# Two edits in a fused graph network: one operation for a complex product, and the sums of h made ahead

## The chip, the cores and the metric

The kernel runs on one core of a Trainium2 chip. The metric is the device time of one execution in microseconds. A core has five engines with instruction queues of their own: TensorE (matmuls; its weight loads are listed apart), VectorE, ScalarE, GpSimd and SyncE, which issues most of the DMA. They are tied together by semaphores. In the profile they are PE, PEld, DVE, ACT, POOL and SP.

## The reference

x has 128 graphs of 128 nodes with 256 channels; everything is float32. Two layers follow each other, and each adds its result to x. Before each, h is the layer norm of x with negative values set to zero.

Layer 0 (the part that the change touches), for each graph:

```python
h1     = relu(bn1(conv1(h)))                   # 1 tap
x_conv = relu(bn2(conv2(h1)) + h)              # 17 taps, 256 -> 256 channels
A      = exp(-dist(h @ w_se.T + b_se)) * mask
x_nmp  = A @ relu(h @ w_msg.T + b_msg)
gi     = concat(x_conv, x_nmp) @ w_ih.T + b_ih
gh     = h @ w_hh.T + b_hh
r, z   = sigmoid(gi_r + gh_r), sigmoid(gi_z + gh_z)
n      = tanh(gi_n + r * gh_n)
x      = x + (1 - z) * n + z * h
```

Layer 1 is a graph convolution over five fixed groups of the first 25 nodes, with 512 hidden channels, twice per group, summed with softmax weights.

## The kernel before, in words

The 128 graphs are worked on in 32 groups q of four. The 17-tap convolution is done by a Fourier transform over pieces of the node axis: F = 48 values a piece, NB = 4 pieces a graph, so that 32 graphs make 128 pieces, one batch. There are four batches of eight groups each.

The work is cut into stages, written as generators.

- **tap_weights** (once) turns the 17 taps of conv2 into 48 matrices of 256x256, by a matmul with the constant `tap` (made on the host in `_fourier`, lines 86 to 89), and stores them in memory as `wfd`. For a frequency f from 1 to 23, slice f and slice 24 + f are the two stored parts of its complex weight.
- **stage_a(q)** normalizes, transposes, makes h (`hTa`, stored in memory as `hTd`), applies conv1 and takes the forward transform into `X`: for each f a real and an imaginary part, X[:, k, 2f] and X[:, k, 2f + 1].
- **stage_b(bat)** multiplies in the frequency domain, for f from 0 to 23 (lines 506 to 530). Frequencies 1 to 23 need a complex product. It is done with three real ones: Xr·Vr and Xi·Vi into the two halves of the PSUM tile `pa`, and (Xr + Xi)·(Vr + Vi) into `pb`. The two sums are made on GpSimd (`add`, lines 494 and 495). ScalarE copies `pa` to SBUF (`pac`, line 519), and three VectorE operations give the real part, Xr·Vr - Xi·Vi, and the imaginary part (lines 523 to 525). `y` goes to memory (`yd`). There are 92 such products.
- **stage_n(q)** loads h of a group, computes the affinity and `x_nmp` (`neighbours`). For the first eight groups this was done ahead, in `early(q)`, beside stage_b(0); for these stage_n only loads the result.
- **stage_c(q)** makes the inverse transform (line 673) and `xc` (lines 676 to 679), and then the gates. The gates' matrix products use a fast scheme with seven products for eight blocks, whose operands are sums of quarter blocks. `sums` (lines 546 to 554) makes four such operands with four VectorE subtractions of 128x256: `th` from h, `tm` from x_nmp, `tc` from xc. They are used from line 730 on. At its end GpSimd combines z, n and h (lines 791 to 796).
- **prepare(blk)** and **block(blk)** are layer 1, for blocks of 16 graphs.

**Order.** Instructions are written out by `Order.run`: it takes steps from lanes of generators, by the lanes' weights and by due times that each step yields. The order of each engine's queue is fixed by it, and an engine runs its queue strictly in order. stage_b(0) runs beside `early` and the folding of the gate weights on GpSimd (`fold_gates`). After that one lane holds stage_n and stage_c of all groups, two at a time; beside it run stage_a and stage_b of the next batches, and when these are through, layer 1.

**Where `th` is made.** Line 759, in stage_c(q) behind the second product with `whn`: if stage_n(q + 1) has ended by then, which sets IN[q + 1], the sums of h for group q + 1 are made there. Otherwise line 665 makes them at the head of stage_c(q + 1), ahead of the operations for `xc`.

**Buffers.** `ptmp` is a ring of five PSUM banks, which `pa`, `pb`, the products of the neighbours (`pse`, `pm`, four `pd`, `px`), the transforms (`ph`, `pc`, `pf`, `pi`, `po`) and layer 1 share, in the order in which they are written out. `pgat` is a ring of three banks for the gates. `hT` has two buffers, `th` one.

Of the kernel before, what the change touches and what calls it, by code (L numbers as in the profile page):

```python
# [9 lines left out]
FP = mybir.dt.float32  # L10
AF = mybir.ActivationFunctionType
ALU = mybir.AluOpType
# [3 lines left out]
B, N, D = 128, 128, 256  # L16
# [3 lines left out]
P = 128  # L20
# [9 lines left out]
NF = F // 2 - 1  # L30
# [29 lines left out]
def _fourier():  # L60

    fwd = np.zeros((P, F, NB))
    inv = np.zeros((P, OB * NB // 2))
    tap = np.zeros((TAPS, F))
    i, t = np.arange(OB), np.arange(TAPS)  # L70
    for b in range(NB):
        for u in range(F):
            n = OB * b + u - PAD
            if 0 <= n < N:
                fwd[n, 0, b], fwd[n, 1, b] = 1, (-1) ** u
                for f in range(1, NF + 1):
                    th = 2 * np.pi * ((f * u) % F) / F
                    fwd[n, 2 * f, b], fwd[n, 2 * f + 1, b] = np.cos(th), -np.sin(th)
    for b in range(NB // 2):
        s = slice(b * OB, (b + 1) * OB)  # L80
        inv[b * F, s], inv[b * F + 1, s] = 1 / F, (-1.0) ** i / F
        for f in range(1, NF + 1):
            th = 2 * np.pi * ((f * i) % F) / F
            inv[b * F + 2 * f, s] = 2 / F * np.cos(th)
            inv[b * F + 2 * f + 1, s] = -2 / F * np.sin(th)
    tap[:, 0], tap[:, NF + 1] = 1, (-1.0) ** t
    for f in range(1, NF + 1):
        th = 2 * np.pi * ((f * t) % F) / F
        tap[:, f], tap[:, NF + 1 + f] = np.cos(th), np.sin(th)
    tap4 = np.zeros((P, 64))  # L90
    for r in range(4):
        tap4[32 * r:32 * r + TAPS, :F] = tap
    return fwd.reshape(P, F * NB), inv, tap4
# [114 lines left out]
def kernel(ctx: ExitStack, tc: tile.TileContext, x, adj, consts, vecs, w_se, conv1_w,  # L208
                    conv2_w, w_msg, b_msg, w_ih, w_hh, W1, W2, b2, fusion_w, out):
    nc = tc.nc  # L210
# [27 lines left out]
    def v(name, i=None):  # L238
        a, b = VAT[name]
        return vec[:, a:b] if i is None else vec[:, a + i:a + i + 1]  # L240
# [109 lines left out]
    xf = lab.enter_context(tc.tile_pool(name="xf", bufs=1, side="right"))  # L350
    LATE = {}
    X = xf.tile([P, 2, F, P], FP, name="X")
# [121 lines left out]
    def stage_b(bat):  # L474
        while not all(q in A_DONE for q in range(bat * BQ, (bat + 1) * BQ)):
            yield 0.0, 0.5
        while "xf" not in LATE:
            yield 0.0, 0.5
        if bat == 0:
            yield 0.0, 12.0  # L480
        WF, xf = {}, LATE["xf"]

        def load_w(f):
            w = WF[f] = xf.tile([P, 2, 3, D], FP, tag="wf", name=f"wf{bat}_{f}")
            for k in range(2):
                nc.sync.dma_start(out=w[:, k, :2], in_=wfd[f::NF + 1, k * P:(k + 1) * P]
                                  .rearrange("s p o -> p s o"))

        XS = {}

        def add(f):

            XS[f] = xf.tile([P, 2, P], FP, tag="xs", name=f"xs{bat}_{f}", bufs=2)
            nc.gpsimd.tensor_tensor(XS[f], X[:, :, 2 * f], X[:, :, 2 * f + 1], ALU.add)  # L494
            nc.gpsimd.tensor_tensor(WF[f][:, :, 2], WF[f][:, :, 0], WF[f][:, :, 1], ALU.add)  # L495

        def product(ps, xk, f, s):

            for k in range(2):
                nc.tensor.matmul(ps, xk(k), WF[f][:, k, s], start=(k == 0), stop=(k == 1))  # L500

        for f in range(2):
            load_w(f)
        yield 0.0, 4.0
        late = None
        for f in range(NF + 1):
            if f + 2 <= NF:
                load_w(f + 2)
            if f < NF:
                add(f + 1)  # L510
            y = xf.tile([P, 2, D], FP, tag="y", name=f"y{bat}_{f}")
            pa = ptmp.tile([P, 2, D], FP, tag="tmp", name=f"pa{bat}_{f}")
            for s in range(2):
                product(pa[:, s], lambda k: X[:, k, 2 * f + s], f, s)
            if f == 0:
                nc.vector.tensor_copy(y, pa)
            else:
                pac = xf.tile([P, 2, D], FP, tag="pac", name=f"pac{bat}_{f}", bufs=2)
                nc.scalar.activation(pac, pa, AF.Copy)  # L519
                pb = ptmp.tile([P, D], FP, tag="tmp", name=f"pb{bat}_{f}")  # L520
                xs = XS.pop(f)
                product(pb, lambda k: xs[:, k], f, 2)
                nc.vector.tensor_sub(y[:, 0], pac[:, 0], pac[:, 1])  # L523
                nc.vector.tensor_add(pac[:, 0], pac[:, 0], pac[:, 1])
                nc.vector.tensor_sub(y[:, 1], pb, pac[:, 0])  # L525
            WF.pop(f)
            if late is not None:
                nc.gpsimd.dma_start(out=yd[bat][:, 2 * f - 2:2 * f], in_=late)
            late = y
            yield 1.7 if f == 0 else 2.6, 1.0  # L530
        nc.gpsimd.dma_start(out=yd[bat][:, F - 2:F], in_=late)
        B_DONE.add(bat)


    IN, IN2, X1, N_DONE = {}, {}, {}, set()

    def load_n(q):
        hT = LATE["io"].tile([P, 2, 512], FP, tag="hT", name=f"hT{q}")
        nc.sync.dma_start(out=hT, in_=hTd[q])
        ad = LATE["io"].tile([P, GB, N], FP, tag="adj", name=f"adj{q}")  # L540
        nc.sync.dma_start(out=ad, in_=adj[q * GB:(q + 1) * GB].rearrange("b n m -> n b m"))
        return hT, ad

    TH = {}

    def sums(name, q, x):


        t = LATE["fr"].tile([P, 4, D], FP, tag=name, name=f"{name}{q}")
        nc.vector.tensor_sub(t[:, 0], x[:, 0, D:], x[:, 0, :D])  # L550
        nc.vector.tensor_sub(t[:, 1], x[:, 1, D:], t[:, 0])  # L551
        nc.vector.tensor_sub(t[:, 2], x[:, 1, D:], x[:, 0, D:])
        nc.vector.tensor_sub(t[:, 3], t[:, 1], x[:, 1, :D])
        return t
# [81 lines left out]
    def stage_n(q):  # L636
        if q < BQ:
            hT = LATE["io"].tile([P, 2, 512], FP, tag="hT", name=f"hT{q}")
            nc.sync.dma_start(out=hT, in_=hTd[q])
            xm = LATE["fr"].tile([P, 2, 512], FP, tag="xnmp", name=f"xms{q}", bufs=2)  # L640
            nc.sync.dma_start(out=xm, in_=xmd[q])
            yield 0.0, 4.0
        else:
            while q not in A_DONE:
                yield 0.0, 1.0
            hT, ad = load_n(q)
            yield 0.0, 4.0
            xm = LATE["fr"].tile([P, 2, 512], FP, tag="xnmp", name=f"xnmp{q}", bufs=2)
            yield from neighbours(q, hT, ad, xm)
        IN[q] = hT, xm  # L650

    def stage_c(q):
        while not (q - 1 in G_DONE and q in IN):
            yield 0.0, 0.5
        hT, xm = IN.pop(q)
# [8 lines left out]

        th = TH.pop(q) if q in TH else sums("th", q, hT)
        xc = fr.tile([P, 2, 512], FP, tag="xc", name=f"xc{q}")
        for h in range(2):
            yt = IN2.pop((q, h))
            s = slice(h * D, (h + 1) * D)
# [19 lines left out]
        def part(ps, w, i, xs, first, last):  # L689


            n = [(m, o) for m in range(w.shape[3] // P) for o in xs]
            for j, (m, (k, x, t)) in enumerate(n):
                nc.tensor.matmul(ps[:, m], w[:, i, k, m * P:(m + 1) * P], factor(i, x, t),  # L694
                                 start=first and j == 0, stop=last and j == len(n) - 1)

        def product(w, i, xs):
            ps = bank(w, i)
            part(ps, w, i, xs, True, True)
            return ps  # L700

        def bank(w, i):
            return pgat.tile([P, w.shape[3] // P, D], FP, tag="gat", name=f"p{w.shape[3]}{q}_{i}")
# [48 lines left out]
        for dc in range(2):  # L752
            pg = pgat.tile([P, 512], FP, tag="gat", name=f"pg{q}_{dc}")
            for k in range(2):
                nc.tensor.matmul(pg, whn[:, k, dc * P:(dc + 1) * P], hT[:, k],  # L755
                                 start=(k == 0), stop=(k == 1))
            nc.vector.scalar_tensor_tensor(r[:, dc], pg, v("b_hh", 4 + dc), r[:, dc],
                                           op0=ALU.add, op1=ALU.mult)
            if dc and q + 1 in IN:
                TH[q + 1] = sums("th", q + 1, IN[q + 1][0])  # L760
            yield 1.75, 0.0

        xs = [(1, xm, tm), (0, xc, tcs)]
# [308 lines left out]
    beside = Lane([tap_weights(), fold_embedding()] + [early(q) for q in range(BQ)])  # L1072
    order.run(begin, beside, until=begin)
    order.run(Lane([stage_b(0)]), beside, Lane([fold_gates()]))
    first, second = [], [setup_1()]
    for bat in range(1, NBAT):
        first += [stage_a(q) for q in range(bat * BQ, (bat + 1) * BQ)] + [stage_b(bat)]
# [47 lines left out]
```

## Time and profile before

| | |
|---|---|
| median of 3 runs | 2251.74 us (2242.12 to 2255.31) |
| span of the profiled run | 2239.3 us, mean granted TensorE clock 0.979 |
| TensorE matmul busy | 2151.1 us |
| TensorE weight loads busy | 1759.6 us |
| VectorE busy | 1332.5 us |
| ScalarE busy | 717.7 us |
| GpSimd busy | 809.7 us |
| matmuls of pa and pb (line 500) | 185.7 + 96.2 us |
| line 519 (ScalarE copy of pa) | 54.7 us |
| lines 523, 524, 525 (VectorE) | 55.3 + 75.6 + 39.1 us |
| lines 550 to 553 for th (VectorE) | 23.9 + 35.6 + 38.9 + 39.0 us |

A group of the profile is read like this: line, engine, operation, output<-inputs by the program's names, shapes and number; then busy time in us and the mean of one in ns; then the idle time of the engine just before these instructions, with what ended most of it. A line of the waits names the waiting instruction, what it waited for, the total in us, the number of waits and the longest. A line of the timeline has the start and the length in us and, in brackets, the idle time before it and its releaser. Every float32 matmul of the program stands in the trace as two records: `pa` has 768 records for 96 tiles of four matmuls.

stage_b(0) runs from about 152 to 277 us, the other three passes of stage_b between 450 and 1355 us; layer 1 begins at about 1390 us.

### The profile page before, as it was taken

The numbers are of one execution on the slowest core, as the hardware profiler recorded it, in microseconds if no ns is written. First come the engines' busy times: TensorE is split into PE (matmuls) and PEld (weight loads), VectorE is DVE, ScalarE is ACT, GpSimd is POOL, SyncE is SP. The second block draws the span as 40 slices with busy tenths as digits, with TensorE's granted clock in tenths as the row PEclk, the third lists the DMA queues.
The fourth block names the chain that finished last, engine by engine and source line by source line (L and its number), as shares of the span: only waits on it lengthen the run. The fifth ranks groups of instructions, "written<-read, shape, count | busy, mean of one in ns | idle before, by whom it ended". The sixth has DMA issues, their size and how long they took to land.

```text
span 2239.3 us, 31926 instructions
## 1 busy us (share of the span) xinstructions
PE 2151.1 (96%) x11820; PEld 1759.6 (79%) x11820; DVE 1332.5 (60%) x2843; ACT 717.7 (32%) x1455; POOL 809.7 (36%) x978
## 2 busy tenths in 40 slices
PE   6998999999999999999999998999999999999997
PEld 3577778888888888888888887787877878878775
DVE  4666755666556676666666665565555565655442
ACT  2431223322234332333332332333233333333232
POOL 2325504365533245542225553423323323222320
PEclk9998999999999999999999999999999999999999
DMA  9886633454533344432325444322222222221221
GB/s 187 240 273 201 199 102 104 146 174 145 161 99 98 92 151 146 140 119 80 100 63 173 137 134 135 77 76 76 76 57 86 67 57 79 80 74 37 74 77 48
DMA packets 193982, 259.72 MB, mean 116 GB/s; under 512 B 21981, under 2 KB 157154, under 8 KB 192290
## 3 DMA queue, kind: packets, MB, share of 16 engines
q1 hardware_dynamic: 165682, 175.89, 27.6%
q0 software_dynamic: 27312, 81.03, 11.7%
q8 instruction: 94, 1.54, 0.3%
q10 hardware_dynamic: 832, 0.75, 0.2%
q14 instruction: 62, 0.51, 0.1%
HBM read 178.44 MB, written 79.17 MB: 115 GB/s over the span
## 4 chain that ended last, share of the span: by engine, by line
PE 81%; DVE 8%; DMA 4%; issue 3%; POOL 2%; ACT 2%; SPq 0%; DVEq 0%; POOLq 0%; ACTq 0%
PE p L694 31%; PE pa L500 6%; PE pg L755 5%; PE ph L996 4%; PE pc L396 4%; PE pz L1005 4%; PE pm L591 4%; PE pi L673 4%; PE pf L409 3%; PE pb L500 3%; PE px L616 2%; PE pg L1038 1%; PE py L979 1%; PE ph L383 1%; PE po L807 1%
## 5 line engine op out<-in xcount | busy, mean ns | idle before, releaser
L500 PE MATMUL pa<-wf,X 128*128 128x256 f32 x768 | 185.7, 385 | 4.6 <-DVE y L525 4.6
L791 POOL TENSOR_TENSOR d<-hT,r 128x512 f32<-128x512 f32 x64 | 86.4, 1350 | 242.1 <-ACT r L788 209.4
L278 POOL TENSOR_TENSOR rs<-rs,cst 128x4 f32<-128x4 f32 x40 | 41.2, 1031 | 361.1 <-DVE rs L277 346.4
L500 PEld LDWEIGHTS pa<-wf,X 128*128 128x128 f32 x768 | 146.9, 193 | 29.4 <-DVE y L525 6.3
L694 PE MATMUL p<-tc,wrz 128*128 128x256 f32 x512 | 153.0, 380 | 4.3 <-DVE tc L551 4.3
L694 PE MATMUL p<-tm,wrz 128*128 128x256 f32 x512 | 152.4, 379 | 1.6 <-DVE tm L551 1.6
L694 PE MATMUL p<-th,wrz 128*128 128x256 f32 x512 | 153.7, 382 | 0.0
L396 PE MATMUL pc<-c1w,hTa 128*128 128x256 f32 x512 | 126.8, 392 | 7.9 <-ACT hTa L385 7.9
L495 POOL TENSOR_TENSOR wf<-wf 128x512 f32<-128x512 f32 x92 | 124.6, 1354 | 13.1 <-DMA wf<-wfd 13.0
L494 POOL TENSOR_TENSOR xs<-X 128x256 f32<-128x256 f32 x92 | 69.5, 755 | 162.5 <-PE pb L500 159.1
L673 PEld LDWEIGHTS pi<-cst,yt 96*128 96x128 f32 x1024 | 123.2, 196 | 4.7 <-issue 3.1
L396 PEld LDWEIGHTS pc<-c1w,hTa 128*128 128x128 f32 x512 | 97.8, 195 | 36.8 <-ACT hTa L385 16.0
L673 PE MATMUL pi<-cst,yt 96*128 96x64 f32 x1024 | 121.8, 278 | 2.9 <-DMA yt<-yd 2.9
L755 PE MATMUL pg<-hT,whn 128*128 128x512 f32 x256 | 122.6, 605 | 0.0
L694 PE MATMUL p<-hT,wrz 128*128 128x256 f32 x384 | 121.7, 400 | 0.0
L591 PE MATMUL pm<-wmsg,hT 128*128 128x256 f32 x512 | 121.7, 382 | 0.0
L519 ACT ACTIVATE pac<-pa 128x512 f32<-128x512 f32 x92 | 54.7, 595 | 198.5 <-PE pa L500 194.9
L996 PE MATMUL ph<-yz,w 128*128 128x96 f32 (+3 forms) x640 | 114.4, 335 | 3.4 <-DVE yz L981 2.8
L523 DVE TENSOR_TENSOR y<-pac 128x256 f32<-128x256 f32 x92 | 55.3, 602 | 104.7 <-ACT pac L519 102.2
L591 PEld LDWEIGHTS pm<-wmsg,hT 128*128 128x128 f32 x512 | 96.7, 191 | 24.0 <-issue 10.8
L694 PEld LDWEIGHTS p<-tc,wrz 128*128 128x128 f32 x512 | 96.7, 190 | 20.0 <-DVE tc L551 7.1
L707 ACT ACTIVATE r<-r,brz 128x256 f32<-128x256 f32 x128 | 58.1, 500 | 168.0 <-DVE r L735 155.4
(205 smaller groups left out, 4864.4 us busy)
## 6 DMA issues: line engine op xcount, KB each, us to landing
wf<-wfd SPq DMA_DIRECT2D x192, 256.0 KB, 3.2
yd<-y POOLq DMA_DIRECT2D x96, 256.0 KB, 2.6
yt<-yd SPq DMA_DIRECT2D x64, 384.0 KB, 3.8
hT<-hTd SPq DMA_DIRECT2D x40, 512.0 KB, 6.0
w<-in_W SPq DMA_DIRECT2D x40, 512.0 KB, 3.8
xa<-in_x SPq DMA_DIRECT2D x128, 128.0 KB, 4.3
hTd<-hTa POOLq DMA_DIRECT2D x32, 512.0 KB, 4.6
xt<-in_x SPq DMA_DIRECT2D x128, 128.0 KB, 3.2
```

The source lines that it names most:

```text
L396: nc.tensor.matmul(pc[:, i], hT[:, k, (2 * h + i) * N:(2 * h + i + 1) * N], c1w[:, k], start=(k == 0), stop=(k == 1))
L409: nc.tensor.matmul(pf[:, i, :F * NB], h1[:, 2 * h + i, k * P:(k + 1) * P], fwd, start=True, stop=True)
L494: nc.gpsimd.tensor_tensor(XS[f], X[:, :, 2 * f], X[:, :, 2 * f + 1], ALU.add)
L495: nc.gpsimd.tensor_tensor(WF[f][:, :, 2], WF[f][:, :, 0], WF[f][:, :, 1], ALU.add)
L500: nc.tensor.matmul(ps, xk(k), WF[f][:, k, s], start=(k == 0), stop=(k == 1))
L591: nc.tensor.matmul(pm[:, i], hT[:, k, j * N:(j + 1) * N], wmsg[:, k], start=(k == 0), stop=(k == 1))
L673: nc.tensor.matmul(pc[:, co, a * 64:(a + 1) * 64], yt[:, a, co * P:(co + 1) * P], inv[:HB], start=True, stop=True)
L694: nc.tensor.matmul(ps[:, m], w[:, i, k, m * P:(m + 1) * P], factor(i, x, t), start=first and j == 0, stop=last and j == len(n) - 1)
L755: nc.tensor.matmul(pg, whn[:, k, dc * P:(dc + 1) * P], hT[:, k], start=(k == 0), stop=(k == 1))
L791: nc.gpsimd.tensor_sub(d, hT[:, dc], r[:, dc])
L996: nc.tensor.matmul(ph, w1[:, k, m * P:(m + 1) * P], yz[:, k, :, o:o + n], start=(k == 0), stop=(k == 1))
L1005: nc.tensor.matmul(pz, w2[:, g, m, cc * P:(cc + 1) * P], hs[g][:, m], start=(m == 0), stop=(m == 3))
```

## The change

The stored weight parts become (Vi - Vr)/2 and -(Vi + Vr)/2, and the index of X in the first two products is swapped. With k = pb = (Xr + Xi)·(sum of the two stored parts), real and imaginary part are then both of the form 2·pa - k. So one `scalar_tensor_tensor` over both halves of `pa`, straight from PSUM, replaces the three VectorE operations, and ScalarE copies `pb` (128x256) to SBUF in place of `pa` (128x512). The matmuls are as many as before and of the same shape.

The second edit is about `th`. A table HT is filled as soon as stage_n has loaded h of a group, and line 759 asks it in place of IN. So the sums of h of the next group are made there also if its neighbours are not through yet.

```diff
     for f in range(1, NF + 1):
         th = 2 * np.pi * ((f * t) % F) / F
-        tap[:, f], tap[:, NF + 1 + f] = np.cos(th), np.sin(th)
+        tap[:, f] = -(np.cos(th) + np.sin(th)) / 2
+        tap[:, NF + 1 + f] = (np.sin(th) - np.cos(th)) / 2
...
             for s in range(2):
-                product(pa[:, s], lambda k: X[:, k, 2 * f + s], f, s)
+                product(pa[:, s], lambda k: X[:, k, 2 * f + (s if f == 0 else 1 - s)], f, s)
             if f == 0:
                 nc.vector.tensor_copy(y, pa)
             else:
-                pac = xf.tile([P, 2, D], FP, tag="pac", name=f"pac{bat}_{f}", bufs=2)
-                nc.scalar.activation(pac, pa, AF.Copy)
                 pb = ptmp.tile([P, D], FP, tag="tmp", name=f"pb{bat}_{f}")
                 xs = XS.pop(f)
                 product(pb, lambda k: xs[:, k], f, 2)
-                nc.vector.tensor_sub(y[:, 0], pac[:, 0], pac[:, 1])
-                nc.vector.tensor_add(pac[:, 0], pac[:, 0], pac[:, 1])
-                nc.vector.tensor_sub(y[:, 1], pb, pac[:, 0])
+                kk = xf.tile([P, D], FP, tag="kk", name=f"kk{bat}_{f}", bufs=2)
+                nc.scalar.activation(kk, pb, AF.Copy)
+                nc.vector.scalar_tensor_tensor(y, pa, 2.0, kk[:, None].to_broadcast([P, 2, D]),
+                                               op0=ALU.mult, op1=ALU.subtract)
...
-    TH = {}
+    TH, HT = {}, {}
...
             yield 0.0, 4.0
+            HT[q] = hT
         else:
             while q not in A_DONE:
                 yield 0.0, 1.0
             hT, ad = load_n(q)
             yield 0.0, 4.0
+            HT[q] = hT
...
-            if dc and q + 1 in IN:
-                TH[q + 1] = sums("th", q + 1, IN[q + 1][0])
+            if dc and q + 1 in HT:
+                TH[q + 1] = sums("th", q + 1, HT.pop(q + 1))
             yield 1.75, 0.0
```

## The prediction

> **What bounds the kernel now.** I read the page's busy shares and slices first, to see which engine sets the end and where it has holes.
>
> ```profile
> span 2239.3 us, 31926 instructions
> PE 2151.1 (96%) x11820; PEld 1759.6 (79%) x11820; DVE 1332.5 (60%) x2843; ACT 717.7 (32%) x1455; POOL 809.7 (36%) x978
> PEclk9998999999999999999999999999999999999999
> ```
>
> TensorE is busy for 96% of the span, VectorE for 60%. Only what shortens TensorE's idle time (2239.3 - 2151.1 = 88 us) or its time at a lower granted clock can pay; VectorE time by itself is free. So I next asked for busy times by stretch, cut at the stages.
>
> ```profile
> 150.00:284.00 134.00, 119.20 (x643) 98.59 (x643) 88.75 (x148) 31.88 (x72) 75.15 (x87) 0.94 0.66 215
> 780.00:960.00 180.00, 180.00 (x953) 153.81 (x952) 124.24 (x229) 56.85 (x110) 92.25 (x106) 0.99 0.46 142
> 960.00:1180.00 220.00, 212.93 (x1172) 183.69 (x1171) 141.30 (x309) 80.94 (x159) 67.22 (x79) 0.98 0.31 94
> 1180.00:1350.00 170.00, 169.89 (x897) 144.67 (x896) 112.67 (x206) 50.42 (x97) 89.26 (x102) 1.00 0.44 139
> 1400.00:2060.00 660.00, 649.22 (x3665) 522.25 (x3664) 383.55 (x812) 215.18 (x450) 195.28 (x237) 0.98 0.25 69
> ```
>
> The columns are the stretch, its length, busy us of PE, PEld, DVE, ACT and POOL, granted clock, DMA share and GB/s. The changed lines of stage_b run in four stretches. In the later ones (780 to 960 and 1180 to 1350 among them) the products of stage_c and the neighbours run beside them and TensorE never rests: nothing is to be had there. The first, 150 to 284, is different: 134 - 119.2 = 14.8 us of idle TensorE and a mean clock of 0.94, some 8 us more. From 1400 to 2060, where stage_b is over, 10.8 us are idle. The waits of TensorE within stage_b(0) say who ends them.
>
> ```profile
> PE pa L500 <- DVE y L525: 4.6, 4, 2.3
> PE pd L603 <- DVE y L525: 3.3, 3, 1.5
> PE pd L603 <- ACT pac L519: 1.9, 3, 0.7
> ```
>
> These are waits for a PSUM bank which the old combination frees late: L525 frees pb's bank, L519 pa's. With 1.1 us behind DVE msg L594, queued behind the same VectorE work, they make 10.9 us. Now the instructions that the change touches, and those I price with.
>
> ```profile
> L519 ACT ACTIVATE pac<-pa 128x512 f32<-128x512 f32 x92 | 54.7, 595 | 198.5 <-PE pa L500 194.9 <-DVE y L525 3.1
> L523 DVE TENSOR_TENSOR y<-pac 128x256 f32<-128x256 f32 x92 | 55.3, 602 | 104.7 <-ACT pac L519 102.2 <-DMA yd<-y 2.4
> L524 DVE TENSOR_TENSOR pac<-pac 128x256 f32<-128x256 f32 x92 | 75.6, 822 | 3.2
> L525 DVE TENSOR_TENSOR y<-pb,pac 128x256 f32<-128x256 f32 x92 | 39.1, 425 | 10.7 <-DVE pac L524 0.9 <-PE ph L383 0.5
> L552 DVE TENSOR_TENSOR th<-hT 128x256 f32<-128x256 f32 x32 | 39.0, 1218 | 0.0
> L552 DVE TENSOR_TENSOR tc<-xc 128x256 f32<-128x256 f32 x32 | 15.2, 477 | 0.0
> L757 DVE SCALAR_TENSOR_TENSOR r<-pg,vec,r 128x512 f32<-128x512 f32 x64 | 47.7, 749 | 49.2 <-PE pg L755 46.1 <-ACT hTa L385 2.0 <-PE ph L383 1.0
> L731 DVE TENSOR_TENSOR u<-u,p 128x512 f32<-128x512 f32 x32 | 22.0, 687 | 39.2 <-PE p L694 39.2
> ```
>
> The same instruction on the same shape costs 477 ns for tc and 1218 ns for th; L523 and L524 are as uneven (up to 3071 ns), while L525, with one input in PSUM, stays within 423 to 426. The timeline of one start of stage_c shows what the slow th does.
>
> ```profile
> 1765.65 1.38 DVE L551 TENSOR_TENSOR th<-hT,th 128x256 f32<-128x256 f32 x1
> ...
> 1768.12 1.44 POOL L791 TENSOR_TENSOR d<-hT,r 128x512 f32<-128x512 f32 x1
> 1768.36 1.48 DVE L553 TENSOR_TENSOR th<-th,hT 128x256 f32<-128x256 f32 x1
> ...
> 1769.76 1.65 DVE L676 SCALAR_TENSOR_TENSOR xc<-pi,s_bn,hT 128x256 f32<-128x256 f32 x4
> ...
> 1770.83 3.05 PE L694 MATMUL p<-xc,wrz 128*128 128x256 f32 x8 [2.65 <-ACT xc L678]
> ```
>
> Each th operation ends just after an operation of GpSimd's tail of the group before; xc (L676) stands behind all four; TensorE waits 2.65 us for xc.
>
> **What the Trainium skill says.** "SBUF — State Buffer", section "Who interferes with whom": a VectorE instruction with two SBUF inputs contends with a GpSimd instruction that reads SBUF, one with at most one SBUF input doesn't. The trace agrees: L525 never stretches, L523, L524 and th do. "TensorE: Matmul & The Clock Gate", section "What's actually happening": the clock halves after an idle window of about 3.4 us. Here the clock falls to 0.72 in 1040 to 1052, 0.81 in 1695 to 1704 and 0.83 in 1766 to 1776, each behind a wait of 2 to 3 us and weak work. "Perfetto Trace Analysis", section "Identifying the Most-Contended Engine", warns that matmul busy time hides headroom; PEld at 79% beside PE at 96% fits, so small stalls beyond the 88 us may exist.
>
> **The change, part by part.**
>
> *Constants and the swapped X index.* The tap table has other values; product still issues four plus two matmuls of the same shape for each f. TensorE work unchanged: 0 us.
>
> *The combination (L519 to L525), 92 times.* Removed: 595 ns of ScalarE, 602 + 822 + 425 = 1849 ns of VectorE. Added: a ScalarE copy of 128x256 from PSUM (v of L768: 378 ns) and one scalar_tensor_tensor of 128x512, pa from PSUM, kk from SBUF. No row shows this very form; the plain L731 (687 ns, one PSUM and one SBUF input) bounds it below, L757 with its per-partition scalar above (749). I take 700, and no stretching, as only one input is in SBUF. VectorE saves 1149 x 92 = 106 us, ScalarE 217 x 92 = 20 us. Nearly all lies beside busy TensorE; what counts is the 10.9 us of bank waits and about half of the 8 us of clock loss in stage_b(0): 7 + 4 = 11 us, taking two thirds of the waits.
>
> *The new wait in it.* kk waits for pb, and the scalar_tensor_tensor for kk, so pa's bank is now held through pb's four matmul records (0.86 us) + 0.38 + 0.70 instead of 0.60: about 1.3 us longer, while pb's comes free some 1.5 us sooner. Behind the waiting VectorE instruction stand msg, ef and aT of the neighbours. Who needs pa's bank soon is pd: it takes four of five banks at once, and where pa and pb were the two tiles before it, its fourth is pa's. Going through the order of PSUM tiles in the trace I find 8 such places, so 0 to 8 x 1.3 = 10 us; I charge 3. Where GpSimd stretches L523 now, the new order is earlier even so. Net for this part: -8 us.
>
> *The sums of h.* HT is filled when hT is loaded, so th(q+1) is made behind L757 of group q for all q. Before, IN was filled only after the neighbours: the first 8 groups, which have none, made th early (0.42 us an operation), the other 24 at the head of stage_c, against GpSimd's d and z (L791 to L794). VectorE time for th falls from 32 x (747 + 1111 + 1218 + 1217) ns = 137 us to at most 32 x 1.81 us (the four tc rows: 419, 443, 477, 475) = 58 us. On the path: xc and all behind it come up to 5 us sooner at 24 heads. TensorE's waits that begin there are p<-xc L678 3.0 us, ph<-yz L981 1.9 us (1400 to 2060) and pc<-hTa L385 4.7 us (960 to 1180, its ScalarE queue stands behind xc): 9.6 us. Three clock drops follow them: 12 x 0.28 + 9 x 0.19 + 10 x 0.17 = 6.8 us. I take 80% of the first and half of the second: -11 us. At its new place th adds 1.7 us to VectorE in front of msg and v2; whn's banks are freed ahead of it, so TensorE isn't held.
>
> Sum: 2251.7 - 8 - 11 = 2232 us.
>
> **The rivals.**
> 1. *All hidden* (no gain beyond noise): TensorE at 180.0 of 180 us speaks for it, the 2 to 3 us waits against. With a quarter of the gain: 2247 us.
> 2. *The longer hold of pa's bank wins* (slower): the gains don't come, 8 places cost 10 us, and half of them bring a clock drop of 3.4 us at half speed (1.7 us each): 2251.7 + 10 + 7 = 2268 us. Against it: L523's stretching, which held the same banks longer, goes.
> 3. *More than the sum*: with 185 us of VectorE gone, small stalls that the busy share hides vanish, and all clock drops at the touched places with them: 11 + 4 + 4 + 10 + 7 = 36 us, 2216 us.
>
> **How the numbers follow.** Forecast 0.52, rival 1 0.26, rival 2 0.08, rival 3 0.14. Half a per cent is 11 us, so faster means under 2240.5: forecast and rival 3 with little lost, 0.66; same takes rival 1 and a little of rival 2, 0.27; slower 0.07. Single times before lie between 2242 and 2255, so the range reaches from rival 3 to just above rival 1: 2212 to 2253.
>
> **What would show it.** Right: th at about 0.42 us in all 32 groups and no L791 beside it; one STT of 0.69 to 0.75 us a step; VectorE near 1150 us; the idle of 150 to 284 under 8 us; p<-xc and pc<-hTa gone from TensorE's waits. Wrong: pd waiting for the new y in its place; kk arriving late behind a full ScalarE queue; clock drops at the same places, which would say that weak matmuls (the 64-column pi), not waits, bring them.

## The result, and the profile after

The changed kernel takes 2218.4 us (median of 4 runs, 2217.09 to 2221.98) against 2248.38 us (4 runs, 2242.12 to 2255.31) beside it: a ratio of 0.9868, 95% interval 0.9834 to 0.9903. A second measurement on another occasion gave 0.9865 (0.9848 to 0.9883). That is 30 us less; 20 had been forecast, within a range that held the time.

The page of the changed kernel, the lines that were shown of before:

```profile
span 2220.1 us, 31670 instructions
PE 2148.5 (97%) x11820; PEld 1760.5 (79%) x11820; DVE 1150.2 (52%) x2659; ACT 701.6 (32%) x1455; POOL 789.2 (36%) x978
PEclk9899999999999999999999999999999999999999
```

VectorE is busy 182 us less (185 had been worked out), TensorE as long as before. The end moved by a sixth of what VectorE saved, so the question is where. The stretches, with the same columns as before (length, busy PE, PEld, DVE, ACT, POOL, granted clock, DMA share, GB/s):

```profile
150.00:284.00 134.00, 125.91 (x753) 107.00 (x752) 64.96 (x121) 34.02 (x89) 76.65 (x90) 0.97 0.76 248
780.00:960.00 180.00, 178.84 (x950) 153.06 (x949) 92.30 (x188) 51.76 (x108) 89.73 (x108) 1.00 0.47 147
960.00:1180.00 220.00, 217.81 (x1227) 189.97 (x1226) 131.76 (x308) 82.03 (x162) 73.60 (x89) 1.00 0.34 105
1400.00:2060.00 660.00, 652.93 (x3687) 526.82 (x3686) 339.67 (x798) 216.58 (x456) 179.94 (x225) 0.98 0.24 69
```

In 150 to 284 us TensorE now does 753 matmul records where it did 643, and is idle for 8.1 us of the 134 in place of 14.8. What it waits for there is no longer the combination; the first three waits, 7.1 us, belong to pi, ph and px, which are no part of it:

```profile
PE pi L675 <- DMA yt<-yd: 3.6, 1, 3.6
PE ph L384 <- DVE xa L284: 1.8, 1, 1.8
PE px L616 <- DVE aT L608: 1.7, 2, 1.0
PE pd L603 <- ACT kk L523: 0.3, 1, 0.3
```

The new pair of instructions, asked for by the tile kk (min, median and max in ns, then who waited for it in us and times):

```profile
L523 ACT ACTIVATE kk<-pb x92: 364/383/385, 170.5 to 1329.5; 128x256 f32<-128x256 f32 x92
L524 DVE SCALAR_TENSOR_TENSOR y<-pa,kk x92: 676/692/693, 170.9 to 1329.9; 128x512 f32<-128x512 f32 x92
...
  DVE y L524: 160.0, 87
...
  PEld pd L603: 1.6, 5
```

One operation of 0.69 us, never stretched, where three took 1.85 us on average. VectorE waits 160 us for kk, but TensorE hardly ever for the pair. And th is quick in all 32 groups; of its 128 operations one, an L550, took longer than 0.43 us (0.91). Two of the four:

```profile
L551 DVE TENSOR_TENSOR th<-hT,th 128x256 f32<-128x256 f32 x32 | 13.6, 425 | 1.1
...
L552 DVE TENSOR_TENSOR th<-hT 128x256 f32<-128x256 f32 x32 | 13.4, 418 | 0.0
```

The head of the same group of stage_c that was shown of before, in the timeline of after:

```profile
1744.50 1.26 POOL L793 TENSOR_TENSOR d<-hT,r 128x512 f32<-128x512 f32 x1
1744.54 1.65 DVE L678 SCALAR_TENSOR_TENSOR xc<-pi,s_bn,hT 128x256 f32<-128x256 f32 x4
...
1745.28 1.69 ACT L680 ACTIVATE xc<-xc,t_bn 128x256 f32<-128x256 f32 x4
...
1748.43 1.89 PE L696 MATMUL p<-xc,wrz 128*128 128x256 f32 x8
```

It is the same head by the order of the matmul records. xc now starts beside GpSimd's d, without four sums ahead of it, and its matmuls start without a wait in brackets.

**Where the time went.** All kernels here but pb_first and both_behind, in which pb is written first, give TensorE the same matmuls in the same order, so the time between the n-th matmul record and the m-th can be set side by side. In brackets is the time lost to the halved clock within the stretch (half of the length at half clock), which comes mostly in multiples of 1.7 us and falls in part differently in each execution. The other rows are the kernels of the experiments below.

```
records          0-750        750-1500     1500-5000   5000-6000   6000-7300   7300-11000
                 start        stage_b(0)                                       layer 1 beside stage_c
before           134.1 (3.4)  160.9 (13.7) 673.0 (1.7) 188.0 (5.1) 257.0 (6.8) 660.9 (10.2)
after            147.3 (15.4) 140.2 (6.8)  674.2 (1.7) 178.4 (0.0) 254.7 (5.1) 661.7 (11.9)
after_again      147.7 (13.7) 138.0 (5.1)  672.5 (0.0) 178.4 (0.0) 253.8 (5.1) 656.2 (8.5)
comb_only        142.4 (11.9) 143.4 (8.5)  671.9 (0.0) 186.8 (3.4) 257.4 (6.8) 661.0 (10.2)
th_only          139.2 (8.5)  162.1 (15.4) 674.3 (1.7) 178.4 (0.0) 255.5 (5.1) 661.6 (11.9)
comb_late        144.8 (11.9) 162.0 (15.4) 676.7 (5.1) 188.0 (5.1) 257.3 (5.1) 657.8 (6.8)
th_behind_xc     145.2 (11.9) 161.5 (15.4) 672.8 (1.7) 178.4 (0.0) 254.6 (6.8) 656.8 (10.2)
three_psum       143.3 (8.5)  144.8 (6.8)  674.9 (3.4) 186.4 (3.4) 257.4 (6.8) 657.8 (6.8)
no_fold          140.1 (8.5)  148.0 (8.5)  674.3 (3.4) 186.6 (3.4) 257.9 (6.8) 657.9 (6.8)
pb_first         138.6 (8.5)  141.1 (6.8)  674.1 (1.7) 180.1 (1.7) 250.4 (1.7) 658.3 (8.5)
comb_behind      149.9 (13.7) 142.0 (6.8)  675.0 (3.4) 178.5 (0.0) 254.6 (5.1) 651.8 (6.8)
both_behind      135.8 (6.8)  140.2 (6.8)  674.7 (3.4) 178.4 (0.0) 255.4 (5.1) 651.9 (5.1)
th_twice         142.4 (10.2) 142.7 (8.5)  677.7 (0.0) 179.9 (0.0) 260.7 (8.5) 663.3 (6.8)
```

From before to after: 20.7 us are gained in records 750 to 1500, 9.6 in records 5000 to 6000, 2.3 in the next stretch, nothing in layer 1. The first gain lies in stage_b(0) itself, which is records 766 to 1349; the stretch goes on some 35 us behind it. From the first matmul of pa to the last of pb the stage took 121.2 us before and takes 99.7: TensorE's idle time in it fell from 12.1 to 0.6 us, its clock loss from 8.5 to 0.

Each row is one execution, but the two gains repeat across the rows. The four kernels with the old combination and the folding in the first pass (before, th_only, comb_late, th_behind_xc) take 160.9 to 162.1 us in records 750 to 1500, all others 138.0 to 148.0. The five that make the sums late, ahead of xc, (before, comb_only, comb_late, three_psum, no_fold) take 186.4 to 188.0 us in records 5000 to 6000, all others 178.4 to 180.1.

The start, which the change leaves alone but for constants, took 134 us in the profiled run of before and 136 to 150 in all others; that is why the two profiled spans differ by 19 us only, and the medians by 30.

### The profile page after: what moved, and what is told of

Its sections match the earlier page's. It is cut to its first block, busy times and chain, and to the rows that moved or that the text cites. A ratio compares the mean times of both kernels' runs of the same rounds, so it can differ in the third digit from the quotient of the medians.

```text
span 2220.1 us, 31670 instructions
## 1 busy us (share of the span) xinstructions
PE 2148.5 (97%) x11820; PEld 1760.5 (79%) x11820; DVE 1150.2 (52%) x2659; ACT 701.6 (32%) x1455; POOL 789.2 (36%) x978
## 4 chain that ended last, share of the span: by engine, by line
PE 84%; DVE 5%; DMA 5%; POOL 2%; issue 1%; ACT 1%; SPq 0%; DVEq 0%; POOLq 0%; ACTq 0%
PE p L696 32%; PE pa L501 7%; PE pg L757 5%; PE pi L675 5%; PE ph L998 4%; PE pz L1007 4%; PE pm L591 4%; PE pc L397 4%; PE pb L501 3%; PE pf L410 3%; PE px L616 2%; PE ph L384 1%; PE pg L1040 1%; DMA xa<-in_x 1%; PE py L981 1%
## 5 line engine op out<-in xcount | busy, mean ns | idle before, releaser
L793 POOL TENSOR_TENSOR d<-hT,r 128x512 f32<-128x512 f32 x64 | 81.3, 1271 | 251.4 <-ACT r L790 218.4
L501 PEld LDWEIGHTS pa<-wf,X 128*128 128x128 f32 x768 | 144.8, 190 | 23.0 <-issue 3.4
L524 DVE SCALAR_TENSOR_TENSOR y<-pa,kk 128x512 f32<-128x512 f32 x92 | 63.6, 691 | 166.0 <-ACT kk L523 160.0
L495 POOL TENSOR_TENSOR xs<-X 128x256 f32<-128x256 f32 x92 | 67.8, 737 | 180.6 <-PE pb L501 178.4
L496 POOL TENSOR_TENSOR wf<-wf 128x512 f32<-128x512 f32 x92 | 116.4, 1265 | 17.6 <-DMA wf<-wfd 17.4
L696 PEld LDWEIGHTS p<-tc,wrz 128*128 128x128 f32 x512 | 96.7, 190 | 20.6 <-DVE tc L551 7.7
L1007 PE MATMUL pz<-hh,w 128*128 128x96 f32 (+3 forms) x640 | 109.4, 325 | 3.5 <-DVE msg L594 1.8
L998 PEld LDWEIGHTS ph<-yz,w 128*128 128x128 f32 x640 | 93.6, 205 | 23.6 <-issue 14.4
```

The source lines that it names most:

```text
L793: nc.gpsimd.tensor_sub(d, hT[:, dc], r[:, dc])
L998: nc.tensor.matmul(ph, w1[:, k, m * P:(m + 1) * P], yz[:, k, :, o:o + n], start=(k == 0), stop=(k == 1))
L1007: nc.tensor.matmul(pz, w2[:, g, m, cc * P:(cc + 1) * P], hs[g][:, m], start=(m == 0), stop=(m == 3))
```

## The experiments

The theory: the two edits gain apart from each other, the combination in stage_b(0) alone, by taking out operations which GpSimd blocked; the sums of h at the heads of stage_c, by letting xc go first. The rivals are that VectorE's saved time counts wherever it is, that the early sums bring it all, or that the longer hold of pa's bank takes part of it.

### Each edit alone

comb_only is the changed kernel with line 759 and HT as before; th_only is the kernel before with the HT lines of the diff.

> The first edit alone: new stored weights, swapped index and the single combining operation; the sums of h stay where they were (made behind the neighbours, for 24 groups at the head of stage_c). Theory (two separate gains, of which the combination's lies in stage_b(0) alone): between the matching matmuls of record 750 and 1250, that is over stage_b(0), some 18 to 21 us are gained, as in the changed kernel, and nothing before or after; ratio to before about 0.991. The size given in the prediction (8 us for this part) would make it 0.996. Rival (the early sums of h bring the gain, also in stage_b(0)): no gain in stage_b(0), ratio 1.000.

Measured 0.9914 (0.9886 to 0.9943). In the table records 750 to 1500 fall to 143.4 us, 17.5 less than before (records 750 to 1250, of which 18 to 21 us were expected, give 16.4), and no other stretch moves by more than the pieces of the clock. The gain is the combination's, and the size in the prediction was too small.

> The second edit alone: HT filled when h is loaded, the old combination of three operations kept. Theory: gains only where the slow sums at the head of stage_c stalled TensorE, about 10 us between 960 and 1180 us and a few from 1400 on, none in stage_b(0); ratio about 0.995 (0.993 to 0.997). Rival (order alone, or the combination is needed to make room for it): under 4 us, ratio above 0.998.

Measured 0.9972 (0.9959 to 0.9985). Records 5000 to 6000 fall by 9.6 us as expected; records 750 to 1500 stay. But from 7300 on nothing comes. The whole is some 6 us, just outside what the theory gave. The product of the two ratios, 0.9886, lies within the interval of both together.

### Does freed VectorE time count where TensorE is never idle?

```diff
-                pac = ...
+                if bat == 0:
+                    pac = ...            # the old combination
...
+                else:
+                    ...                  # the new one
```

> The kernel before with the new combining operation in batches 1 to 3 only, batch 0 with the old one, and the old stored weights in all, so that the products of batches 1 to 3 are combined from parts of the other form and aren't the convolution; the instructions and their sizes are those of the two kernels. Theory (in the later three passes of stage_b TensorE is never idle, so VectorE time freed there is hidden): same as before, ratio 0.999 to 1.001, though VectorE is busy some 75 us less. Rival (the saving counts in every pass): three quarters of the gain of the combination, ratio about 0.993.

Measured 1.0019 (1.0002 to 1.0036), with VectorE busy 1265.6 us in place of 1332.5. Taking 67 us off VectorE in three of the four passes gains nothing; it is, if anything, 0.2% slower. The stretches 1500 to 5000 and 6000 to 7300, in which these passes lie, are longer by 3.7 and 0.3 us, the first with 3.4 us more of clock loss. The rival is out.

### Blocking, or the number of operations?

```diff
-                nc.vector.tensor_sub(y[:, 0], pac[:, 0], pac[:, 1])
-                nc.vector.tensor_add(pac[:, 0], pac[:, 0], pac[:, 1])
+                nc.vector.tensor_sub(y[:, 0], pa[:, 0], pac[:, 1])
+                nc.vector.tensor_add(pac[:, 0], pa[:, 1], pac[:, 0])
```

> The kernel before with its three combining operations kept, but the first two read pa in PSUM where they read its copy, so that each has one input in SBUF; ScalarE's copy stays. VectorE work is then 3 x 0.42 = 1.27 us a step, in place of 1.85 before and 0.69 with the single operation. Theory (what stalled stage_b(0) were operations with two SBUF inputs, blocked for up to 3 us by GpSimd): L523 and L524 within 0.43 us each, and three quarters or more of the gain of the single operation, ratio 0.991 to 0.994. Rival (the number of operations and the freed VectorE time bring it): half of it or less, ratio 0.996 to 0.999.

Measured 0.993 (0.9903 to 0.9957). The groups of this kernel:

```profile
L523 DVE TENSOR_TENSOR y<-pa,pac 128x256 f32<-128x256 f32 x92 | 39.0, 424 | 122.2 <-ACT pac L519 116.1 <-DMA yd<-y 6.0
L524 DVE TENSOR_TENSOR pac<-pa,pac 128x256 f32<-128x256 f32 x92 | 38.1, 414 | 0.0
```

Three operations are kept, and 602 and 822 ns become 424 and 414 because one input now comes from PSUM. Records 750 to 1500 take 144.8 us: 16.1 of the 17.5 us that the single operation gains alone. In stage_b(0) itself VectorE is busy 79.9 us before, 59.3 here and 47.5 with the single operation alone: taking out the stretching, 20.6 us, brought most of the gain, taking out operations, another 11.8 us, little. So most of it is the blocking; by the whole times, whose intervals overlap, the share isn't known closely. What is left shows in the waits of this kernel in the same stretch, pa's bank being read by two operations:

```profile
PE pd L603 <- DVE pac L524: 3.2, 5, 1.5
```

Who blocks was tried from the other side, on the kernel before:

```diff
-                nc.gpsimd.tensor_tensor(w[:, dst], w[:, a], w[:, b], op)
+                if dst in (2, 5, 6):
+                    nc.gpsimd.memset(w[:, dst], 0.03)
...
-            nc.gpsimd.tensor_scalar(w[:, 3], w[:, 3], -1.0, None, op0=ALU.mult)
```

> The kernel before without GpSimd's arithmetic in the folding of the gate weights, which runs beside stage_b(0); it leaves the gate weights wrong: three of seven parts are filled with a constant, which only writes, the others stay as loaded. Everything else is the kernel before. Theory of blocking: the 2 to 3 us operations of L523 and L524 in stage_b(0) were blocked behind these 768-element operations (1.8 us each), so they go, and a third to two thirds of the combination's gain comes, ratio 0.993 to 0.997, all between 150 and 284 us. Rival (the sums for xs and wf, which stay, do the blocking, or the number of operations counts): no gain, ratio 0.999 or more.

Measured 0.9929 (0.9903 to 0.9956), and records 750 to 1500 take 148.0 us, 12.9 less: some three quarters of the combination's gain, more than expected. The waits for the combination are down from 9.8 us to 5.8 in this stretch:

```profile
PE pa L500 <- DVE y L525: 4.6, 4, 1.7
...
PE pd L603 <- DVE y L525: 1.0, 1, 1.0
...
PE pd L603 <- ACT pac L519: 0.2, 1, 0.2
```

So GpSimd's folding costs TensorE time. But the way that was expected for it is not borne out: taken together, L523 and L524 are no shorter without it. What became shorter is lr of the neighbours, another operation with two SBUF inputs (two parts of ef) in the same queue. Over the whole program, first lr before, then the three in this kernel:

```profile
L582 DVE TENSOR_TENSOR lr<-ef 128x256 f32<-128x256 f32 x32 | 26.8, 839 | 16.8 <-ACT ef L579 16.8
...
L524 DVE TENSOR_TENSOR pac<-pac 128x256 f32<-128x256 f32 x92 | 81.5, 886 | 3.2
L523 DVE TENSOR_TENSOR y<-pac 128x256 f32<-128x256 f32 x92 | 47.7, 518 | 101.8 <-ACT pac L519 99.4 <-DMA yd<-y 2.3
L582 DVE TENSOR_TENSOR lr<-ef 128x256 f32<-128x256 f32 x32 | 17.4, 543 | 16.8 <-ACT ef L579 16.8
```

L523 and L524 together take 35.6 us in stage_b(0), 35.8 before; lr takes 5.9 us in place of 15.4. This fits a VectorE queue that was late as a whole: relieving it at either place brought most of the gain. In comb_only lr still takes up to 5.56 us, and TensorE hardly waits. The sums for xs and wf, which are GpSimd's other work there, stretch the combination without the folding too. Nor does the stretching alone tell why the first pass is the one that hurts: L523 and L524 together take 1.56 us a step there, and 1.27 to 1.47 in the later passes, where taking them out gains nothing (comb_late).

### The new wait: pa's bank and kk

```diff
+            if f:
+                pb = ...                 # product for pb and kk, as in the changed kernel
             pa = ptmp.tile([P, 2, D], FP, tag="tmp", name=f"pa{bat}_{f}")
```

> The changed kernel with the product for pb and its copy written ahead of those for pa, so that kk is there before pa is through and pa's bank is held some 1.3 us less. Theory (in the changed kernel the longer hold of pa's bank and the wait for kk cost nothing that is left): same as the changed kernel, ratio to before 0.984 to 0.989. Rival (the new wait does cost, as the prediction charged 3 us): 3 us better, and VectorE's idle time behind kk (160 us now) falls to a third. A risk: pb then waits for GpSimd's sum of the weights at the head of a step.

Measured 0.9863 (0.9837 to 0.9889), as the changed kernel. kk is there in time now (idle time before the new operations, and before who waited, in us and times):

```profile
  PE pb L501: 157.3, 61
  PE pa L501: 89.3, 45
...
  ACT kk L518: 11.7, 10
```

VectorE's wait for kk falls from 160.0 to 11.7 us and records 750 to 1500 take 141.1 us, as after (140.2 and 138.0). The wait that the change adds costs TensorE nothing that can be seen; the interval is some 6 us to either side.

### Why the early sums gain: sooner, shorter, or out of xc's way?

```diff
-        th = TH.pop(q) if q in TH else sums("th", q, hT)
+        th = TH.pop(q, None)
...
             load_yt(q + 1, h)
+            if h and th is None:
+                th = sums("th", q, hT)
```

> The kernel before, with the sums of h, where they are made late, put behind the operations for xc in place of ahead of them; they still run against GpSimd's tail and are still slow. Theory (what cost time is that xc and the ScalarE queue behind it stood behind the slow sums): most of the gain of the early sums, ratio 0.994 to 0.997. Rival (what cost time is the stretched VectorE work itself, wherever it stands): no gain, ratio 0.999 or more.

Measured 0.9929 (0.9908 to 0.995), better than the early sums alone. A head of stage_c in this kernel:

```profile
1761.66 1.65 DVE L676 SCALAR_TENSOR_TENSOR xc<-pi,s_bn,hT 128x256 f32<-128x256 f32 x4
...
1764.56 1.37 DVE L551 TENSOR_TENSOR th<-hT,th 128x256 f32<-128x256 f32 x1
...
1765.56 1.89 PE L696 MATMUL p<-xc,wrz 128*128 128x256 f32 x8
...
1767.27 1.48 DVE L553 TENSOR_TENSOR th<-th,hT 128x256 f32<-128x256 f32 x1
```

The sums shown are as slow as before (1.37 and 1.48 us, beside GpSimd's tail). Over all groups th takes 115 us, against 137 before and 54 at the early place; and nothing waits for it. Records 5000 to 6000 take 178.4 us, to the tenth what the early sums give. So what gained there is neither making them sooner nor making them faster, but letting xc go first. The waits that the prediction named at these heads are, in the kernel before, the first in records 5000 to 6000, the others in layer 1:

```profile
PE pc L396 <- ACT hTa L385: 4.7, 2, 2.8
...
PE p L694 <- ACT xc L678: 3.0, 2, 2.6
PE ph L996 <- DVE yz L981: 1.9, 1, 1.9
```

The four long ones among them (2.8, 1.9, 2.6 and 1.9 us) stand at the same matmul records in all five kernels with late sums ahead of xc and in none of the eight others. With clock losses taken off, layer 1 (7300 to 11000) takes 650.7 to 651.1 us in the five kernels with the late sums, 647.7 to 649.8 in the four with early ones (th_twice, below, apart), 645.0 to 646.8 in the three with sums behind xc.

One reason why the early place does less well in layer 1 shows in the timeline of the changed kernel:

```profile
1603.24 2.77 POOL L896 TENSOR_SCALAR x1h<-x1h 128x1024 f32<-128x1024 f32 x1 [1.59 <-DVE x1h L284]
...
1603.65 0.91 DVE L550 TENSOR_TENSOR th<-hT 128x256 f32<-128x256 f32 x1
...
1605.60 0.68 DVE L594 TENSOR_TENSOR msg<-pm,bmsg 128x512 f32<-128x512 f32 x1
...
1606.34 1.15 PE L1007 MATMUL pz<-hh,w 128*128 128x112 f32 x8 [1.75 <-DVE msg L594]
```

msg stands behind the sums, its PSUM bank comes free late, and TensorE waits 1.75 us. This wait stands in all four kernels with early sums and in none with late ones or with sums behind xc; it is 1.8 us of the some 3 us that separate them from the latter in layer 1. To weigh that place, the four operations were put in it twice:

```diff
                 TH[q + 1] = sums("th", q + 1, HT[q + 1])
+                x, t = HT.pop(q + 1), TH[q + 1]
+                nc.vector.tensor_sub(t[:, 0], x[:, 0, D:], x[:, 0, :D])
...
```

> The changed kernel with the four early sums of h made twice in the same place, with the same values, 1.7 us more VectorE work for each group in front of msg. Theory (the early place costs in layer 1 because it stands ahead of msg, whose lateness then holds TensorE): 3 to 8 us slower than the changed kernel, all of it in records 7300 to 11000. Rival (VectorE has room there, and the early place costs nothing): within 2 us of the changed kernel.

Measured 0.9917 (0.9901 to 0.9934) against 0.9865 (0.9848 to 0.9883) for the changed kernel beside it: 12.5 us slower, more than expected. The wait that was looked for nearly doubles,

```profile
PE pz L1012 <- DVE msg L594: 3.2, 1, 3.2
```

and with three smaller ones TensorE's waits for msg come to 5.2 us in place of 1.8. But the loss is not in layer 1 alone, as the theory had it: against after it is 3.5 us in 1500 to 5000, 1.5 and 6.0 in the next two stretches, and 1.6 in layer 1 (6.7 with clock losses taken off). So VectorE work at this place costs, in layer 1 and ahead of it; how much of what the single sums cost there comes from msg was not settled.

### Both edits in the better form

comb_behind is the single operation with the sums behind xc; both_behind has pb first besides. after_again is the changed kernel, for comparison.

> The single combining operation together with the sums of h behind the operations for xc (in place of early). Theory (two separate gains, and the place of the sums matters only in that xc comes ahead of them): the product of the two ratios measured apart, 0.9914 x 0.9929 = 0.984, as fast as the changed kernel (0.987) or up to 6 us faster, since the early place put VectorE work ahead of msg. Rival (early is better, the difference of the two kernels with one edit was chance): 0.987 to 0.991.

> The changed kernel once more, so that the two versions built on it can be set against it on the same chip. Every theory: ratio to before 0.984 to 0.990; stage_b(0), records 750 to 1500, in 140 to 144 us; records 5000 to 6000 in 178 to 180 us; layer 1 beside stage_c, records 7300 to 11000, in 658 to 663 us, as the kernel with early sums alone had it.

> The single combining operation with pb ahead of pa, and the sums of h behind xc in place of early. Theory (behind xc is the better place in layer 1 by 4 to 9 us; pb ahead of pa changes little): ratio 0.981 to 0.986, records 7300 to 11000 in 650 to 656 us. Rival (the difference between the places was chance): as the changed kernel, 0.984 to 0.990, and 658 us or more in that stretch.

Measured: comb_behind 0.9846 (0.9819 to 0.9874), in the forecast range, but not clear of the changed kernel; beside each other after_again 0.9865 (0.9848 to 0.9883) and both_behind 0.9822 (0.9804 to 0.9839), 2207.2 us against 2217.5, which is clear of it. Layer 1 takes 651.8 and 651.9 us, against 656.2 and 661.7 for the two executions of the changed kernel. The second execution missed its own expectation in two stretches (138.0 us for 140 to 144, 656.2 for 658 to 663), so a single stretch of one execution is not good to better than some 6 us; the clock losses account for most of that. Not all of the 10 us between the last two is placed: in the profiled runs 12 us are in the start, which differs by chance, 4 in layer 1. comb_behind has the sums behind xc without pb first, and its interval reaches to both, so how the 10 us divide between the two was not settled.

## Why the prediction came out as it did

**Right in kind.** VectorE's 182 us are hidden but for two places; stage_b(0) and the heads of stage_c are these two; the later passes of stage_b give nothing (comb_late); TensorE's waits for xc (3.0 us), for hTa between 960 and 1180 us (4.7 us), for y and for pac are gone. Of the signs named, only the idle time of 150 to 284 us fell short, at 8.1 us for under 8. That the forecast total came to two thirds of the measured one owes something to luck, since two errors of opposite sign partly cancelled: alone, the combination gained 19 us (13 to 26) where 8 were taken, the early sums 6 us (3 to 9) where 11 were.

**Mis-sized: the term "7 + 4 = 11 us" for stage_b(0), less the charge of 3.** It measured 20.7 us in records 750 to 1500. The two causes were right, the fractions taken of them too small: two thirds of the waits were taken (7 of 10.9 us), and TensorE's idle time in stage_b(0) fell by 11.5, to 0.6 us; half of the clock loss was taken (4 of 8 us), and all 8.5 us went. The prediction used the Trainium skill's "SBUF — State Buffer", section "Who interferes with whom" (a VectorE instruction with two SBUF inputs contends with a GpSimd instruction that reads SBUF), for the operations' own durations and went no further. three_psum shows that this interference was the cause of most of the stage's idle time: with three operations kept and one input of each in PSUM, it fell from 12.1 to 4.0 us. One L523 of the kernel before is the example: it took 3.07 us, behind three GpSimd operations in a row. They are in the timeline of the kernel before, VectorE's line first, then GpSimd alone:

```profile
187.76 3.07 DVE L523 TENSOR_TENSOR y<-pac 128x256 f32<-128x256 f32 x1 [1.18 <-ACT pac L519]
...
186.84 1.81 POOL L329 TENSOR_TENSOR wrz<-wrz 128x768 f32<-128x768 f32 x1
188.60 0.73 POOL L494 TENSOR_TENSOR xs<-X 128x256 f32<-128x256 f32 x1
189.29 1.25 POOL L495 TENSOR_TENSOR wf<-wf 128x512 f32<-128x512 f32 x1
```

**Too high: the charge of 3 us for pa's bank.** pd waits 0.3 us for kk, and pb_first, which shortens the hold, gains nothing that can be seen.

**The term of the sums, 11 us:** 9.6 us came in records 5000 to 6000, of which 5.1 were clock losses, and 2.3 after them; th_only as a whole measured 6 us (3 to 9). All the waits named went. Of the three clock drops, those behind records 5330 and 8830 stand in all five kernels with late sums ahead of xc and in no other; the third, behind 9196, stands in the kernel before alone, though the other four wait there as long, so the wait alone doesn't bring it. What was missing is the gain in layer 1, where waits of 4.9 us went and, with clock losses taken off, 1 to 3 us came, against 4 to 6 with the sums behind xc. The step that failed is "At its new place th adds 1.7 us to VectorE in front of msg and v2; whn's banks are freed ahead of it, so TensorE isn't held": whn's banks are free, but msg's is not, and the new wait of 1.8 us takes back part of what the old ones (p<-xc, ph<-yz) gave; where the rest went stays open.

**The price of the new operation** (700 ns, between 687 and 749) measured 691, kk 383 for 378.

**Rival 3** (2216 us) was the nearest in time, and in stage_b(0) for the reason that it gave: the small stalls and the clock losses there went nearly whole. Rivals 1 and 2 didn't come.

## What to carry to other kernels

When the same VectorE instruction on the same shape has two durations, look for what GpSimd does beside it: moving one input to PSUM took the stretching away without taking out an operation. Time saved on an engine that is off the path pays only where its lateness holds the bounding engine, so ask what stands behind a slow instruction in its queue; putting it behind the one that others wait for gained at least as much as making it earlier and two to three times faster. And work made earlier is placed in front of something: see whose bank or buffer that something frees.

## What the runs showed of the hardware that was not expected

- A VectorE operation with two SBUF inputs is not always let in between two GpSimd operations: L523 (0.42 us by itself) took 3.07 us, from 187.76 to 190.83, while three GpSimd operations ran from 186.84 to 190.54; lr (0.42 us by itself) took up to 5.56 us. th, against the operations of GpSimd's tail, took turns with them instead, at 1.48 us each. GpSimd itself loses little: its sum for wf took 1354 ns on average before and 1265 in the changed kernel.
- A scalar_tensor_tensor with a constant from PSUM and SBUF, 128x512, takes 691 ns, as a plain tensor_tensor (687); with a per-partition scalar it is 749.
- Clock losses at the start of the program, in code that all kernels share, vary from 3.4 to 15.4 us between executions, a spread of 12 us beside the 30 us that this change gains.
- A clock drop did not need a wait as long as the idle window of about 3.4 us that the prediction takes from the Trainium skill ("TensorE: Matmul & The Clock Gate", section "What's actually happening"): the drops behind records 5330 and 8830 follow waits of 2.8 and 1.9 us, each just behind the 64-column matmuls of pi. The kernels without these waits run the same pi matmuls there without a drop, so there the wait is needed. But in the kernel before a drop also followed pi without any wait (at 870, 986 and 1932 us), so it isn't always needed; what share the light matmuls have in these drops was not tried.
